# Block 0's two token halves issued together, its second gather behind the first, and all other loads held until the second half has landed

## The chip, the cores and the metric

The kernel runs on one core of one Trainium2 chip. The metric is the device time of one execution in microseconds (us). A core has five engines that each run their own instructions in order: TensorE (PE; its weight loads are shown as PEld), VectorE (DVE), ScalarE (ACT), GpSimd (POOL) and SyncE (SP). SP and GpSimd issue the transfers (DMAs) between the chip's large memory and the core's own; sixteen DMA engines carry them out. Engines wait for one another and for transfers by semaphores.

## The reference

There are 64 sequences of 64 tokens with 1024 numbers each (4096 tokens, 32-bit floats). Two layers with a residual are applied:

```
x = x + (x B[id0]^T) A[id0]                    # rank-16 adapter of the sequence, one of 64
logits = x Wr^T + 5 * onehot(id1)              # 8 experts
gates  = softmax of the top 2 logits, else 0
h      = x A1^T                                # 8 experts x rank 16 = 128 numbers
x = x + x W^T + 2 * (h * gates) B1
```

`W` is 1024 x 1024 and costs most of the arithmetic.

## The kernel before

The tokens stand in the large memory with the features outermost (`xT`). The kernel takes them in eight blocks k of 512 tokens; a block is two tiles `x(k,0)` and `x(k,1)` of 512 features each (1 MB). Two blocks make a super-block s, and the product with `W` plus the identity (which brings the residual) is made for a super-block with Strassen's scheme in two levels: seven outer products of quarter matrices, each in turn from seven inner ones, so that sums of tokens (`t`, `ti`) and of weights (`m`, `s`) are formed ahead of the matmuls. In super-block 0 the first outer product is made without the inner level (`pw`). The combined weights are written to the large memory (`s_kept`) in super-block 0 and read back by the other three.

Ahead of the products each block goes through these steps, all with the names that the profile shows:

- `gather` (GpSimd, indirect DMA): the block's adapter rows, `gb` (of `in_b`) and `ga` (of `in_a`), 0.5 MB each.
- `turn`: transposes of `gb` on TensorE (`pt`), copied by ScalarE to `bt`.
- `project`: `pb` from `bt` and the tokens, in two steps, one for each half of the features; VectorE masks it to `bx`.
- `adapt`: `px` from `ga` and `bx`, which VectorE adds to the tokens (`x<-px,x`).
- `rows`: `ph` from the tokens and `a1_sb` (expert rows and router), copied to `h` by ScalarE.
- `gates`: some twenty small VectorE operations from `l<-h,bias` to the gated rows `h<-h,s`.
- `weigh`: transposes of the gated rows (`pg`), copied to `hg`; the products read it with `b1_sb`.

The order of the instructions on every engine is made when the kernel is built. Each step is handed to `Plan.add` with the engines that it may run on, an estimated duration, what it reads and writes, a due time `at`, and for a transfer its size `kb`. `Plan.order` plays the steps through with these estimates and always takes, on the engine that can start first, the ready step that is due first. `LAND`, `KB` and `GATHER` are its estimates for transfers:

```
if st["kb"]:
    moved = max(moved, clock[e]) + st["kb"] / self.KB
    end[n] = (moved if e == "SP" else clock[e] + self.GATHER) + self.LAND
```

`behind` is a condition of the planner alone: the step is placed after the start of another. A real hold is made in another way: a small GpSimd copy writes one column of the tile that a transfer will fill, so that the transfer has to wait for that copy, and the copy reads from a tile that has to land first. The kernel before has two of them. In `load`, the tile `x(0,1)` is held by a copy from `x(0,0)`, whose load is cut into two transfers of 0.5 MB. In `consts`, `a1_sb` is held by a copy from `gb` of block 0. SP issues its transfers in order, so all that is planned behind `a1` waits with it. GpSimd runs in order too, so a gather that stands behind such a copy waits as well. The transfers of SP share eight semaphores in turn, and one of them can be issued only when the transfer eight places earlier has landed.

SP's order at the start is: the ids of the first layer, `x(0,0)` in two parts, `wr` (the router) and `ids1` (the ids of the second layer, one row sent to all partitions), `x(0,1)`, `a1`, two of the sixteen pieces `w(i,j)` of `W`, `x(1,0)`, `x(1,1)`, the other fourteen (first `w(1,0)` and `w(1,1)`), `b1`. GpSimd's is: gather `gb(0)`, hold of `x(0,1)`, gather `ga(0)`, copy of `wr` into `a1_sb`, hold of `a1_sb`, gathers `gb(1)` and `ga(1)`, then sums of weights. The list of calls is:

```
for k, at in ((0, -60), (1, -42)):
    load(k, 0, at)
    gather(k, "gb", b0, at - 1)
    load(k, 1, at)
    gather(k, "ga", a0, at)
    if k == 0:
        consts()
```

Of the kernel before, what the change touches and what calls it, by code (L numbers as in the profile page):

```python
# [14 lines left out]
P = 128  # L15
# [18 lines left out]
class Plan:  # L34
# [10 lines left out]
    LOOK = 0.2  # L45
    LAND = 1.8
    KB = 350.0
    GATHER = 1.5
    AHEAD = 6.0
    PACE = {"DVE": 0.36, "POOL": 0.73}  # L50
    SET = {"SP": 1.2, "DVE": 3.1, "POOL": 2.9}
# [13 lines left out]
    def order(self):  # L65
# [65 lines left out]
        while ready:  # L131
# [23 lines left out]
# [3 lines that stand above are left out]
            where[n] = e  # L158
# [23 lines left out]
def kernel(  # L182
# [52 lines left out]
    TB = 512  # L235
# [5 lines left out]
    HC = NC // 2  # L241
# [15 lines left out]
    act, pool, sp = Pinned(tc, nc.scalar), Pinned(tc, nc.gpsimd), Pinned(tc, nc.sync)  # L257
# [6 lines left out]
    plan = Plan(slots, {"l"})  # L264
# [7 lines left out]
    def new(tag, shape, name):  # L272
        return pools[tag].tile(shape, F32, tag=tag, name=name)
# [24 lines left out]
    a1_sb = const.tile([P, NC, P + E], F32, name="a1_sb")  # L298
# [13 lines left out]
    def consts():  # L312
        plan.add({"SP": 0.4}, lambda e: sp.dma_start(wr_c, wr), [], [("wr_c",)], -53, kb=8)
        plan.add(
            {"SP": 0.4}, lambda e: sp.dma_start(ids1_sb, ids1[0:1, :].to_broadcast([P, NB])),
            [], [("ids1",)], -53, kb=32,
        )

        def hold(e):

            pool.tensor_copy(a1_sb[:, 0, :1], made["gb", 0][:, :1])

        plan.add({"POOL": 0.2}, hold, [(("gb", 0),)], [("a1",)], -56)
        plan.add({"SP": 0.4}, lambda e: sp.dma_start(a1_sb[:, :, :P], a1), [], [("a1",)], -45, kb=512)
        plan.add({"SP": 0.4}, lambda e: sp.dma_start(b1_sb, b1), [], [("b1",)], -29, kb=512, behind=[("a1",)])

        def spread(e):
            pool.tensor_copy(a1_sb[:, :, P:], wr_c)

        plan.add({"POOL": 0.3}, spread, [("wr_c",)], [("wr",)], -45)  # L330
# [24 lines left out]
    made = {}  # L355

    def part(t, cs=range(HC), gs=range(NG)):
        return [(t, c, g) for c in cs for g in gs]
# [7 lines left out]
    def load(k, i, at):  # L366
        t = ("x", k, i)

        held = (k, i) == (0, 1)

        def hold(e):

            made[t] = new("q", [P, HC, TB], f"x_{k}_{i}")
            pool.tensor_copy(made[t][:, 0, :1], made["x", 0, 0][:, 0, :1])


        cuts = ((0, HC // 2), (HC // 2, HC)) if (k, i) == (0, 0) else ((0, HC),)

        def fn(c0, c1):
            if not held and c0 == 0:  # L380
                made[t] = new("q", [P, HC, TB], f"x_{k}_{i}")
            sp.dma_start(
                made[t][:, c0:c1],
                xT[(i * HC + c0) * P : (i * HC + c1) * P, k * TB : (k + 1) * TB].rearrange(
                    "(c p) t -> p c t", p=P
                ),
            )

        if held:
            plan.add(  # L390
                {"POOL": 0.2}, hold, part(("x", 0, 0), [0]), part(t), at, [("q", t)]
            )
        for c0, c1 in cuts:
            plan.add(
                {"SP": 0.5}, lambda e, c0=c0, c1=c1: fn(c0, c1),
                [], part(t, range(c0, c1)), at, [("q", t)] * (not held and c0 == 0),
                kb=256 * (c1 - c0), behind=[("a1",)] * (k == 1) + [(t, 0, 0)] * (c0 > 0),
            )

    def gather(k, tag, table, at):  # L400
        def fn(e):
            made[tag, k] = new(tag, [P, D], f"{tag}_{k}")
            pool.indirect_dma_start(
                out=made[tag, k],
                out_offset=None,
                in_=table,
                in_offset=bass.IndirectOffsetOnAxis(ap=idx[:, k : k + 1], axis=0),
            )

        plan.add(  # L410
            {"POOL": 1.1}, fn, [], [((tag, k),)], at, [(tag, (tag, k))], kb=512,
            behind=[(("x", 0, 1), 0, 0)] * ((tag, k) == ("ga", 0)) + [("a1",)] * (k == 1) + [(("px", 1, 1, 0),)] * (k > 1),
        )

    def turn(k, g, at):
# [261 lines left out]
    POOL = {"POOL": 1.25}  # L677
# [367 lines left out]
# [7 lines that stand above are left out]
# [9 lines left out]
    for s in range(NSUP):  # L1061
        k0 = 2 * s
        a0_ = s * SLOTS
        if s == 0:
            late(0, -14)
        late(k0 + 1, a0_ + 4 * (s > 0))
        token_sum(s, 3, a0_ + 3)
        token_sum(s, 2, a0_ + 5)
        token_sum(s, 4, a0_ + (25 if s == 0 else 7))
        token_sum(s, 1, a0_ + 20)  # L1070
        products(s)
        if s + 1 < NSUP:
            k0, k1 = k0 + 2, k0 + 3
            gather(k0, "gb", b0, a0_ + 8)
            gather(k0, "ga", a0, a0_ + 9)
            load(k0, 0, a0_ + 9)
            load(k0, 1, a0_ + 14)
            early(k0, a0_ + 17)
            late(k0, a0_ + 23)
            gather(k1, "gb", b0, a0_ + 22)  # L1080
            gather(k1, "ga", a0, a0_ + 23)
            load(k1, 0, a0_ + 22)
            load(k1, 1, a0_ + 29)
            early(k1, a0_ + 32)
# [48 lines left out]
```

## Time and profile before

| | |
|---|---|
| median of 3 runs | 521.96 us (521.91 to 522.75) |
| the profiled execution | 521.59 us, span 519.8 us, granted TensorE clock 1.00 |
| busy: PE, PEld | 504.9 us (97%), 439.3 us (85%) |
| busy: DVE, ACT, POOL | 300.9 us (58%), 41.1 us (8%), 170.0 us (33%) |
| bytes moved | 99.19 MB, mean 191 GB/s |
| first matmul | starts at 9.72 us |

The span runs from the first to the last instruction of the profiled execution; times in the lines of the profile count from its start. A line of the timeline or of the chain of waits begins with start and duration; a group of equal instructions is drawn together, with its count. Nearly all instructions stand under line 29, since one helper issues them, so they are told apart by their tiles. In a list of waits, the numbers are the total, the count and the longest. In the lines by DMA queue, q1 carries what SP issues and q0 the gathers; the numbers are packets, MB, and the time that the packets took as a share of sixteen engines.

### The profile page before, as it was taken

The page shows a single profiled execution, that of the slowest core. Times are in us where ns is not written, and L with a number is a line of the kernel's source. Part 1 is how long each engine was busy: PE and PEld are TensorE (multiplying, and loading weights), DVE is VectorE, ACT ScalarE, POOL GpSimd, SP SyncE. Part 2 cuts the span into 40 slices and gives each one's busy share as a digit, 9 for nine tenths or more (in the row PEclk, how much of TensorE's full clock was granted, in tenths as well). Part 3 has the DMA queues.
Part 4 walks back from the last instruction along what each step waited for, and adds up shares of the span by engine and source line. Part 5 has one row for each costly group of instructions (what it writes and reads, how often), then busy time and mean ns, then how long its engine had stood idle before and what let it go on. Part 6 is the DMA issues. An engine that isn't in the chain of part 4 may idle for free.

```text
span 519.8 us, 8542 instructions
## 1 busy us (share of the span) xinstructions
PE 504.9 (97%) x3432; PEld 439.3 (85%) x3432; DVE 300.9 (58%) x572; ACT 41.1 (8%) x81; POOL 170.0 (33%) x141
## 2 busy tenths in 40 slices
PE   2999999999999999999999999999999999999996
PEld 2857988888888988898888998889888898888885
DVE  0699998986953383526684256435486418433632
ACT  1111100002000100012000100000200010000000
POOL 4072067170332144124233313312423322433300
PEclk9999999999999999999999999999999999999999
DMA  7999276799566269716565537744546633610122
GB/s 263 370 367 381 103 263 221 276 326 342 194 202 203 63 194 317 238 61 204 182 224 186 159 101 212 269 149 124 163 161 202 204 95 107 204 62 0 56 104 83
DMA packets 54247, 99.19 MB, mean 191 GB/s; under 512 B 4928, under 2 KB 11072, under 8 KB 54208
## 3 DMA queue, kind: packets, MB, share of 16 engines
q1 hardware_dynamic: 51904, 90.26, 51.6%
q0 software_dynamic: 2304, 8.39, 4.8%
q8 instruction: 27, 0.44, 0.3%
q14 instruction: 12, 0.10, 0.0%
HBM read 69.01 MB, written 29.62 MB: 190 GB/s over the span
## 4 chain that ended last, share of the span: by engine, by line
PE 96%; DMA 2%; DVE 0%; issue 0%; SPq 0%; POOL 0%
PE pa L29 39%; PE pb L29 38%; PE ph L29 11%; PE px L29 3%; PE pw L29 3%; DMA x<-in_xT 2%; PE pt L29 1%; PE pg L29 1%; DVE o L29 0%; SPq L29 0%; DVE bx L29 0%; POOL x L29 0%
## 5 line engine op out<-in xcount | busy, mean ns | idle before, releaser
L29 PE MATMUL pa<-ti,s 128*128 128x256 f32 x432 | 102.5, 380 | 0.0
L29 PE MATMUL pb<-ti,s 128*128 128x256 f32 x384 | 95.8, 380 | 0.0
L29 PEld LDWEIGHTS pa<-ti,s 128*128 128x128 f32 x432 | 80.8, 190 | 11.2 <-issue 0.2
L29 PEld LDWEIGHTS pb<-ti,s 128*128 128x128 f32 x384 | 72.1, 190 | 10.0
L29 PEld LDWEIGHTS ph<-a_sb,x 128*128 128x128 f32 x512 | 62.6, 190 | 1.5 <-issue 0.4
L29 PE MATMUL ph<-a_sb,x 128*128 128x136 f32 x512 | 63.1, 279 | 0.2 <-issue 0.2
L29 POOL TENSOR_TENSOR ti<-x,ti 128x512 f32<-128x512 f32 x24 | 32.2, 1340 | 78.0 <-PE pb L29 77.1
L29 DVE TENSOR_TENSOR o<-pb,o 128x512 f32<-128x512 f32 x47 | 32.4, 690 | 36.1 <-PE pb L29 21.7
L29 PE MATMUL pa<-x,s 128*128 128x256 f32 x216 | 51.9, 379 | 0.0
L29 POOL TENSOR_TENSOR ti<-t,ti 128x512 f32<-128x512 f32 x18 | 25.7, 1429 | 71.0 <-PE pb L29 61.3
L29 POOL TENSOR_TENSOR ti<-x 128x512 f32<-128x512 f32 x24 | 30.8, 1282 | 55.4 <-PE pb L29 41.8
L29 PEld LDWEIGHTS pa<-x,s 128*128 128x128 f32 x216 | 40.1, 190 | 5.3 <-issue 0.3
L29 DVE TENSOR_TENSOR x<-px,x 128x512 f32<-128x512 f32 x64 | 39.8, 684 | 6.8 <-PE px L29 6.8
L29 PE MATMUL pa<-t,s 128*128 128x256 f32 x168 | 41.0, 380 | 0.0
L29 POOL TENSOR_TENSOR ti<-t 128x512 f32<-128x512 f32 x18 | 24.4, 1358 | 42.9 <-PE pb L29 33.4
L29 PEld LDWEIGHTS pa<-t,s 128*128 128x128 f32 x168 | 31.6, 190 | 4.5 <-issue 0.4
L29 DVE TENSOR_TENSOR o<-pa,u 128x512 f32<-128x512 f32 x32 | 22.0, 688 | 20.8 <-PE pa L29 20.1
L29 DVE TENSOR_TENSOR u<-pb,u 128x512 f32<-128x512 f32 x21 | 14.5, 689 | 25.1 <-ACT u L29 20.7
L29 POOL TENSOR_TENSOR s<-w,w 128x512 f32<-128x512 f32 x12 | 17.0, 1418 | 36.0 <-DVE w L29 36.0
L29 PE MATMUL pb<-hg,b_sb 128*128 128x256 f32 x96 | 28.6, 379 | 0.0
L29 DVE TENSOR_TENSOR o<-pa,v 128x512 f32<-128x512 f32 x15 | 10.3, 690 | 25.9 <-PE pa L29 25.9
L29 DVE TENSOR_TENSOR v<-pa,u 128x512 f32<-128x512 f32 x16 | 11.0, 689 | 22.3 <-PE pa L29 22.1
(113 smaller groups left out, 609.5 us busy)
## 6 DMA issues: line engine op xcount, KB each, us to landing
s<-s_kept SPq DMA_DIRECT2D x147, 256.0 KB
x<-in_xT SPq DMA_DIRECT2D x15, 1024.0 KB
out_T<-o SPq DMA_DIRECT2D x30, 512.0 KB
s_kept<-s SPq DMA_DIRECT2D x28, 256.0 KB
s_kept<-w SPq DMA_DIRECT2D x18, 256.0 KB
w<-in_w SPq DMA_DIRECT2D x16, 256.0 KB
x<-in_xT SPq DMA_DIRECT2D x2, 512.0 KB
out_T<-o SPq DMA_DIRECT2D x4, 256.0 KB
```

What stands on the lines that cost most here:

```text
L29: return self._tc.keep_in_program_order(f(*args, **kwargs))
```

## The change

`x(0,0)` is loaded by one transfer instead of two, and the load of `x(0,1)` loses its hold, so that both are issued one after the other. The gather `ga(0)` is no longer placed behind the start of `x(0,1)`. The hold on `a1_sb` copies from `x(0,1)` instead of `gb(0)`, so what is queued behind it waits until that half has landed. The planner's estimate for a gather goes from 1.5 to 3.0. In the built order GpSimd now issues `ga(0)` right behind `gb(0)`, then the hold, the copy of `wr`, `gb(1)`, `ga(1)`; SP issues `x(0,0)`, `x(0,1)`, `wr`, `ids1`, `a1` and the rest as before.

The instructions of every engine are otherwise the same in number, but the plan orders some of them anew. Up to about 65 us these differ: on VectorE, the identity added to `w(1,1)` stands ahead of block 0's gates, and in block 1 all four `ti` and one `o` stand ahead of the gates, not after them; on TensorE, block 0's `pg` and the first `pa` stand ahead of block 1's second `px`, the first `pb` of product 2 ahead of block 1's `ph`, and block 1's `pg` behind block 2's `pt`. Later than that, the orders are the same but for two stores that change places.

```diff
-    GATHER = 1.5
+    GATHER = 3.0
...
         def hold(e):
 
-            pool.tensor_copy(a1_sb[:, 0, :1], made["gb", 0][:, :1])
-
-        plan.add({"POOL": 0.2}, hold, [(("gb", 0),)], [("a1",)], -56)
+            pool.tensor_copy(a1_sb[:, 0, :1], made["x", 0, 1][:, 0, :1])
+
+        plan.add({"POOL": 0.2}, hold, part(("x", 0, 1), [0]), [("a1",)], -56)
...
     def load(k, i, at):
         t = ("x", k, i)
 
-        held = (k, i) == (0, 1)
-
-        def hold(e):
-
+        def fn(e):
             made[t] = new("q", [P, HC, TB], f"x_{k}_{i}")
-            pool.tensor_copy(made[t][:, 0, :1], made["x", 0, 0][:, 0, :1])
-
-
-        cuts = ((0, HC // 2), (HC // 2, HC)) if (k, i) == (0, 0) else ((0, HC),)
-
-        def fn(c0, c1):
-            if not held and c0 == 0:
-                made[t] = new("q", [P, HC, TB], f"x_{k}_{i}")
             sp.dma_start(
-                made[t][:, c0:c1],
-                xT[(i * HC + c0) * P : (i * HC + c1) * P, k * TB : (k + 1) * TB].rearrange(
+                made[t],
+                xT[i * HC * P : (i + 1) * HC * P, k * TB : (k + 1) * TB].rearrange(
                     "(c p) t -> p c t", p=P
                 ),
             )
 
-        if held:
-            plan.add(
-                {"POOL": 0.2}, hold, part(("x", 0, 0), [0]), part(t), at, [("q", t)]
-            )
-        for c0, c1 in cuts:
-            plan.add(
-                {"SP": 0.5}, lambda e, c0=c0, c1=c1: fn(c0, c1),
-                [], part(t, range(c0, c1)), at, [("q", t)] * (not held and c0 == 0),
-                kb=256 * (c1 - c0), behind=[("a1",)] * (k == 1) + [(t, 0, 0)] * (c0 > 0),
-            )
+        plan.add(
+            {"SP": 0.5}, fn, [], part(t), at, [("q", t)], kb=1024, behind=[("a1",)] * (k == 1)
+        )
...
         plan.add(
             {"POOL": 1.1}, fn, [], [((tag, k),)], at, [(tag, (tag, k))], kb=512,
-            behind=[(("x", 0, 1), 0, 0)] * ((tag, k) == ("ga", 0)) + [("a1",)] * (k == 1) + [(("px", 1, 1, 0),)] * (k > 1),
+            behind=[("a1",)] * (k == 1) + [(("px", 1, 1, 0),)] * (k > 1),
         )
```

## The prediction

> **What bounds the kernel now.** I read the table of busy time first: TensorE (PE) 504.9 of 519.8 us. Then TensorE's waits, for the whole span:
>
> ```profile
> PE pt L29 <- DMA gb<-in_b,idx: 9.7, 1, 9.7
> PE pb L29 <- DMA x<-in_xT: 0.6, 1, 0.6
> PE px L29 <- DVE bx L29: 0.4, 1, 0.4
> PE ph L29 <- issue: 0.2, 1, 0.2
> ```
>
> All four lie in the first 19 us; from `ph` on TensorE never waits again. So the end moves by what the start gains and by any new hole later, one for one. The chain of waits gives the start:
>
> ```profile
> 4.78 8.80 DMA x<-in_xT
> 13.59 0.14 issue
> 13.72 1.11 PE pb L29 x32
> 14.86 0.30 DVE bx L29
> 15.20 2.07 PE px L29 x64
> 17.27 1.18 PE pt L29 x8
> ...
> 18.64 7.65 PE ph L29 x64
> ```
>
> Block 0's second half x(0,1), held until the first quarter of tokens has landed, takes 8.8 us for 1 MB. GpSimd's timeline gives the gathers of block 1, which the change delays:
>
> ```profile
> 9.64 0.18 POOL L29 COPY a_sb<-gb 128x1 f32<-128x1 f32 x1 [2.95 <-DMA gb<-in_b,idx]
> 9.97 0.97 POOL L29 DMA_INDIRECT gb<-in_b,idx  x1
> ```
>
> The list of transfers gives gb(0) 6.7 us from issue to landing, gb(1) 6.4, each ga 8.0: gb(0) lands at 9.58, gb(1) at 16.37, ga(0) at 12.92. Why x(0,1) is slow shows in the DMA split by queue between 5.3 and 8 us (145 GB/s in all, 353 in the three us before):
>
> ```profile
> DMA packets 282, 0.39 MB, mean 145 GB/s; under 512 B 195, under 2 KB 195, under 8 KB 282
> ...
> q0 software_dynamic: 84, 0.34, 54.4%
> q1 hardware_dynamic: 198, 0.05, 7.4%
> ```
>
> The 256-byte rows of wr and ids1 stand in SP's queue ahead of x(0,1) and trickle for 2.7 us; none of x(0,1) moves before 8.
>
> A second place matters because the order written after the change differs there, between 40 and 65 us. VectorE (DVE) and TensorE meet:
>
> ```profile
> 44.53 2.48 DVE L29 TENSOR_TENSOR x<-px,x 128x512 f32<-128x512 f32 x4
> ...
> 54.74 0.19 DVE L29 TENSOR_TENSOR l<-h,bias 128x32 f32<-128x32 f32 x1
> ...
> 63.11 0.69 DVE L29 TENSOR_TENSOR w<-m,w 128x512 f32<-128x512 f32 x1
> ...
> 63.86 1.70 PEld L29 LDWEIGHTS pa<-t,w 128*128 128x128 f32 x8
> ```
>
> VectorE is busy almost without a gap, and the combined weights that `pa` loads at 63.86 are finished at 63.80. Nothing is spare at that point.
>
> **What the skill says.** "DMA: Bandwidth & Descriptors", section Queues, rings and completion order: each DMA engine goes round its queues packet by packet. The trace agrees: from 10.5 to 12 us q0 (4 KB packets) and q1 (2 KB) moved 103 and 116 packets, so the gathers took 0.40 of 0.62 MB. The same page, Anatomy of one DMA, fits a GpSimd transfer as 2.0 us plus bytes over 436 GB/s, 3.2 us for a 0.5 MB gather; the trace has 6.4 to 8.0, and I use the trace. "SBUF — State Buffer", section Who interferes with whom: a VectorE operation with two SBUF inputs contends with GpSimd operations that read SBUF. The trace agrees: a `l<-s,l` of 0.19 us (56.09) takes 1.28 at 28.59 beside a GpSimd sum.
>
> **Part by part.**
>
> 1. *x(0,0) as one load, x(0,1) right behind, no hold.* Removes one SP issue (0.46 us), one GpSimd copy (0.18). x(0,1) is issued near 1.7 instead of 4.78; wr and ids1 move behind it, 0.4 us later at SP. GpSimd is free, so ga(0) goes at about 4.1 instead of 4.92. x(0,1) now shares the rings with gb(0) from 5.3 on, when q0's first packets appear. One DMA engine's share of both halves is 64 packets of 2 KB; 16 engines at 400 GB/s need 2.1/0.40 = 5.3 us, begun at 2.4. Add gb(0)'s 0.52/0.41 = 1.3 us and part of ga(0): last packets 9.0 to 10.3, landing some 0.9 later (the tail that x(0,1) shows now, thinning from 12.5, landing at 13.59). I take **10.6** (9.9 to 11.3), 3 us earlier than now.
>
> 2. *gb(0) without the trickle.* ga(0) today needs about 3.2 us from first packets (about 9.7) to landing against 2 KB packets; gb(0) begun at 5.3 then lands at **8.5**, not 9.58. TensorE: `pt` 8.6; `pb`'s first half 1.87 later as now (9.72 to 11.59), 10.5; it takes 1.54, to 12.0. The second half needs x(0,1), there since 10.6: no wait. 1.12, then 0.34 for `bx`: `px` starts at **13.5** instead of 15.20 and ends at 15.5. It needs ga(0): queued behind gb(0), about 8.7 plus 3.2, plus up to 1 us for the trickle that now falls on it: 12 to 13, just covered.
>
> 3. *Other loads held until x(0,1) has landed.* The hold on `a1_sb` moves from gb(0)'s landing (9.64) to x(0,1)'s (10.65). Queued behind it on GpSimd: the copy of wr (which used to run at 6.45, 0.24 us), gb(1), ga(1); on SP: a1, two w, x(1,0), x(1,1), fourteen more w, b1. gb(1) is issued at 10.65 + 0.34 (hold to next issue, as 4.58 to 4.92) + 0.24 = **11.2** instead of 9.97. Its landing: 2.4 to first packets (as gb(0), 2.88 to 5.3) plus 3.2, or today's 6.4 to 6.7. I take 5.7: **16.9** (16.3 to 17.9). TensorE runs in order, so block 1's `pt` stands after `px` and waits from 15.5 until 16.95, where it started at 17.20. **Gain 0.25 us**, not the 1.7 that `px` gains. `ph` follows by 1.4 as now. a1 needs to land by 18.4; it is issued at 10.9, 1.1 later than now, and behind the trickle: hidden by `pt`'s wait.
>
> 4. *Block 1's tokens and w.* The DMA pause of 5.3 to 8 is exchanged for one from about 10.3 to 12.5. x(1,1) is needed at about 27. SP issues the w that waits for its semaphore at 26.45 now; I take the same, cover 0.7 us. w(1,1), which SP's issue at 27.97 shows landed just before, now stands on VectorE ahead of `l<-h,bias` (26.75): that gate chain starts near 28.4 and is drawn into GpSimd's eight sums. Counted by hand with the durations at 28.6 to 38.7, `h` is gated at 41.2 instead of 40.3. `pg` at 43.4 covers that; if w(1,1) is over 0.7 us later, no longer.
>
> 5. *GATHER 3.0 reorders 40 to 65 us.* `pg` (0.54) and `pa` (1.62) move ahead of block 1's second `px`, and six `pb` (2.5) ahead of `ph`. TensorE's sum is the same, but VectorE's `x<-px,x` can start only after them. TensorE: 43.34 + 0.54 = 43.9, `pa` to 45.5, its result at 45.9; VectorE takes it (0.6), `m` (0.6), so `x<-px,x` starts at **47.1**, not 44.53. From there with the rows now: four adds 2.5, eight token sums 4.8, four `ti` 2.6, one `o` 0.6: `l<-h,bias` at 57.6 (54.74 now). Gates and gated rows 4.6, `o`, `m` and two `w` 2.7: **64.9**, against 63.8 now, where two `ti` and the `o` (1.9) stood after the gates. `pa` waits for it: **a loss of 1.05 us** (0.6 if a gap of VectorE is counted twice; 1.8 if item 4's cover fails). The `pg` before it waits 0.6 of that. Later order is the same, with both engines shifted alike.
>
> Sum: −0.25 + 1.05 = **+0.8 us**. The profiled execution is 521.59 (span 519.8), 0.37 under the median 521.96, which I move: **522.7**. A difference under 0.2%, 1.04 us, can't be told from no change here.
>
> **Rivals.**
>
> - *A, likeliest (0.47):* as summed, most of the early gain used up by the wait for gb(1), the rest and more by VectorE's order. 520.9 to 523.0. Against it: the landing times carry 0.7 us of doubt.
> - *B, slower (0.38):* gb(1) keeps its 6.7 us and x(0,1) lands at 11.3, since the gathers take two packets' bytes for each of its own. gb(1) is issued at 11.9, lands at 18.6: `pt` 1.4 later than now, plus 1.05: +2.5, 524.4. It decides from a gb(1) landing of 17.2 on, where the start gains nothing and +1.05 remains. For it: no gather in the trace took under 6.4. Against it: gb(0) suffered from the trickle, gb(1) stood behind ga(0); both reasons go.
> - *C, faster (0.15):* VectorE has slack that I miss, for instance GpSimd's sums overlapping less, so that item 5 costs nothing, and gb(1) lands at 15.5 to 16. Then −1.2 to −1.7: 520.5. The full −1.7 is the limit: `px` ends no earlier than 15.5. Against it: 63.80 beside 63.86.
> - *D:* the change doesn't bring x(0,1) earlier, because SP's queue is served late: it needs x(0,1) after 13; then B's sum and more. Included in B.
>
> **Numbers.** Faster 0.15, same 0.47, slower 0.38. The range leaves out B's tail and the extreme of C: 520.9 to 524.1. A alone with its own doubts: 522.0 to 523.0.
>
> **What would show it.** Right: x(0,1) landed near 10.6 and no wait of `pb` for x; `px` near 13.5; a new wait of `pt` for gb of 1 to 2 us, ending near 17; a wait of `pg` or `pa` for VectorE at 62 to 65 us. Wrong: block 1's `pt` right after `px` (item 3), or no TensorE wait after 40 us (item 5), or a wait of `pb` for block 1's x at 27 (item 4).

## The result, and the profile after

The changed kernel took 526.84 us (median of six, 525.49 to 527.78) beside 521.93 us for the kernel before: a ratio of 1.0088, 95% interval 1.0070 to 1.0106. It is 4.9 us slower, outside the range that was forecast (520.9 to 524.1). A second series of the same kernel (`a2_again`, 17 times) gave 525.50 beside 521.70, ratio 1.0073 (1.0053 to 1.0093); eleven of those times lie between 523.5 and 525.7, six between 526.7 and 527.7. The two profiles, of a 527.78 us execution and of one of 524.96 us, show both kinds.

The list of TensorE's waits, for the longer of the two (total, count, longest):

```profile
PE pt L29 <- DMA gb<-in_b,idx: 14.1, 2, 10.8
PE px L29 <- DVE bx L29: 0.4, 1, 0.4
```

Before, `pt` waited once, 9.7 us. Now it waits twice: 10.8 us for block 0's `gb` and 3.3 us, which is new, for block 1's. The wait of `pb` for tokens is gone. The chain of waits (start, duration, what) says where the second wait comes from:

```profile
2.21 10.29 DMA wr_c<-in_wr
12.49 0.05 issue
12.55 0.24 POOL a_sb L29
12.79 0.15 issue
12.93 8.36 DMA gb<-in_b,idx
21.29 0.14 issue
21.43 1.77 PE pt L29 x8
23.20 8.51 PE ph L29 x64
31.71 1.88 PE pb L29 x64
```

Block 1's `pt` starts at 21.43, 17.20 before. Its gather lands 8.36 us after its issue (6.4 before), and the issue itself, 9.97 before, is at 12.93. GpSimd's timeline has the reason, in the brackets (idle before, and what ended it):

```profile
11.72 0.18 POOL L29 COPY a_sb<-x 128x1 f32<-128x1 f32 x1 [6.49 <-DMA x<-in_xT]
12.55 0.24 POOL L29 COPY a_sb<-wr_c 128x64 f32<-128x64 f32 x1 [0.64 <-DMA wr_c<-in_wr]
12.93 0.97 POOL L29 DMA_INDIRECT gb<-in_b,idx  x1
```

The hold is released at 11.72 (9.64 before). Behind it stands the copy of `wr`, which has to wait for `wr` to land, and only then comes the gather. (In what follows, `pt(1)`, `pb(1)` and so on are the steps of block 1.)

`pt` and `ph` are also longer than before, 1.77 and 8.51 us against 1.18 and 7.65. The split by stretches (start and end, length, busy PE, PEld, DVE, ACT, POOL, then the granted TensorE clock, DMA share, GB/s) shows the clock at half from about 21.6 to 25.0:

```profile
20.00:21.00 1.00, 0.00 (x0) 0.00 (x0) 1.00 (x3) 0.00 (x0) 0.00 (x0) 1.00 1.04 412
21.00:22.00 1.00, 0.57 (x4) 0.61 (x5) 1.00 (x2) 0.00 (x0) 0.00 (x0) 0.81 1.02 387
22.00:23.00 1.00, 1.00 (x6) 0.80 (x4) 0.92 (x5) 0.56 (x1) 0.00 (x0) 0.50 1.04 401
...
25.00:26.00 1.00, 1.00 (x11) 1.00 (x10) 1.00 (x2) 0.00 (x0) 0.00 (x0) 0.98 1.05 368
```

The Trainium skill, page "TensorE: Matmul & The Clock Gate", Part 1: The HAM clock gate, states that TensorE falls to half its clock after about one window of 3.4 us without work and needs about as long at work to come back. This trace agrees: 3.3 us of waiting, a fall 3.5 us after TensorE's last work (18.14), then 3.4 us at 0.50.

In the other profile, `a2_again`, TensorE's timeline has a shorter wait and no fall:

```profile
16.68 2.07 PE L29 MATMUL px<-bx,ga 32*128 32x128 f32 x64 [0.38 <-DVE bx L29]
19.83 1.07 PE L29 MATMUL pt<-ident,gb 128*128 128x128 f32 x8 [1.08 <-DVE x L29]
```

There `gb(1)` was issued at 12.75 and landed at 19.69, 0.14 before `pt` started. The list puts this wait down to VectorE, one of whose additions ended just then; but `pt(1)` starts 0.13 or 0.14 after the landing in `after`, `e2_old_order` and `e5_cut` too, and where the gather had landed earlier (`e6_copy_behind`, `e13_copy_old_order`) it doesn't wait for the additions. In the longer one fifteen of the sixteen DMA engines had finished `gb(1)` by 20.26 and the last came at 21.29.

That the fall of the clock goes with the long times shows in more than these two profiles. The mean granted clock of every execution is on record: 0.995 to 0.997 in the ten executions of 526.7 us or more of the two series, 0.998 to 1.000 in the thirteen shorter ones.

Two points on TensorE sum the whole span up: the start of block 1's `pb` (all that the start costs lies ahead of it) and the time from there to the first `pa<-x,s` (the order of 40 to 65 us lies in it). The last four rows are kernels of the next section.

| kernel | start of pb(1) | from there to `pa<-x,s` | span |
|---|---|---|---|
| before | 26.22 | 39.72 | 519.8 |
| after | 31.64 (+5.42) | 40.42 (+0.70) | 526.0 (+6.2) |
| a2_again | 28.82 (+2.60) | 40.43 (+0.71) | 523.2 (+3.4) |
| e1_order | 26.14 (-0.08) | 40.79 (+1.07) | 521.1 (+1.3) |
| e2_old_order | 28.66 (+2.44) | 39.70 (0.0) | 522.3 (+2.5) |
| e6_copy_behind | 27.25 (+1.03) | 40.42 (+0.70) | 521.6 (+1.8) |
| e13_copy_old_order | 27.78 (+1.56) | 39.71 (0.0) | 521.4 (+1.6) |

In every row the two differences add up to that of the span within 0.1 us, but for `e1_order`, where 0.3 us lie later. So there are two costs in the changed kernel: the start, 2.6 to 5.4 us, and the order, 0.7.

### The profile page after: what moved, and what is told of

It reads as the page before. It is cut to its first block, busy times and chain, and to the rows that moved or that the text cites. A ratio compares the mean times of both kernels' runs of the same rounds, so it can differ in the third digit from the quotient of the medians.

```text
span 526.0 us, 8534 instructions
## 1 busy us (share of the span) xinstructions
PE 507.3 (96%) x3432; PEld 441.2 (84%) x3432; DVE 298.0 (57%) x572; ACT 40.9 (8%) x81; POOL 169.4 (32%) x140
## 4 chain that ended last, share of the span: by engine, by line
PE 95%; DMA 4%; SPq 0%; DVE 0%; issue 0%; POOL 0%
PE pa L29 39%; PE pb L29 37%; PE ph L29 11%; PE px L29 3%; PE pw L29 3%; DMA wr_c<-in_wr 2%; DMA gb<-in_b,idx 2%; PE pt L29 1%; PE pg L29 1%; SPq L29 0%; DVE o L29 0%; POOL a_sb L29 0%
## 5 line engine op out<-in xcount | busy, mean ns | idle before, releaser
L29 PEld LDWEIGHTS pa<-ti,s 128*128 128x128 f32 x432 | 80.7, 190 | 11.2 <-issue 0.2
L29 POOL TENSOR_TENSOR s<-w,w 128x512 f32<-128x512 f32 x12 | 17.0, 1419 | 35.5 <-DVE w L29 20.9
L29 PE MATMUL pb<-x,s 128*128 128x256 f32 x96 | 23.9, 381 | 0.0
```

Of the source, the lines that this page charges most:

```text
L29: return self._tc.keep_in_program_order(f(*args, **kwargs))
```

## The experiments

All were timed beside the kernel before on the same chip; ratios are to it, with 95% intervals. The diffs show the lines that matter: the text behind a # names the experiment, and "..." stands for code that is left out.

**The two costs apart: e1_order, e2_old_order.**

```diff
-    GATHER = 1.5          # e1: the kernel before with the new order alone
+    GATHER = 3.0
-    GATHER = 3.0          # e2: the changed kernel with the old order
+    GATHER = 1.5
```

> The kernel before with GATHER = 3.0 as the only edit: TensorE and ScalarE take the changed kernel's order, all loads and gathers stay as before. Theory T (the start costs most: block 1's gather comes late, TensorE waits 3.3 us for it and then runs 3.4 us at half clock; the order adds little): pa waits some 0.4 us for VectorE's combined weights and starts 0.7 us later than before, 522.6 us in all (+0.7; the prediction said +1.05). Rival R (the order of 40 to 65 us is the cause): +3 us or more. Rival 0 (the order costs nothing, the 0.7 us seen comes from the shifted start): 522.0.

> The changed kernel with GATHER = 1.5 again: the engines' orders of the kernel before, the new loads and holds. Theory T: gb(1) still lands near 21.3, pt of block 1 waits over 3 us, the granted clock falls to half at 22 to 25 us, pb(1) starts 5.4 us later than before; in all about +4.2 over the kernel before, 526.1. Rival R (the order): back to about 522.

Measured: 522.86 (+1.3; ratio 1.0027, 1.0014 to 1.0040) and 524.94 (+3.4; 1.0066, 1.0051 to 1.0082). The sum is 4.6; the change cost 4.9 and, in its second series, 3.8. The order is a cost of its own, though in e1_order VectorE takes one `m` behind block 1's gates that the changed kernel takes ahead of them. TensorE's waits in e1_order name it:

```profile
PE pa L29 <- DVE w L29: 0.6, 1, 0.6
```

Rival R falls. In e2's profile, of its shortest time, `gb(1)` landed at 19.53 and the clock did not fall, against the expectation; as in `a2_again`, a short time goes without it.

**When gb(1) is issued: e3_gathers_first, e6_copy_behind.**

```diff
-            behind=[("a1",)] * (k == 1) + [(("px", 1, 1, 0),)] * (k > 1),     # e3
+            behind=[(("px", 1, 1, 0),)] * (k > 1),
-        plan.add({"POOL": 0.3}, spread, [("wr_c",)], [("wr",)], -45)          # e6
+        plan.add({"POOL": 0.3}, spread, [("wr_c",)], [("wr",)], -45, behind=[(("ga", 1),)])
```

(In e6 the line is called after block 1's gathers are in the plan.)

> The changed kernel with block 1's two gathers no longer behind the hold on a1 (GpSimd issues gb(0), ga(0), gb(1), ga(1), then the hold and the copy of wr); the other loads stay held until x(0,1) has landed. Theory T (it is the time at which gb(1) is issued): gb(1) lands before 16, no wait of pt over 1 us, no fall of the clock, and pb(1) starts within 1 us of the kernel before; what stays is the order's 0.7 us and x(0,1) landing 1 to 2 us later for the added gather bytes: about 523 (+0.5 to +1.5). Rival H (the hold on the other loads, a1 and w coming late, costs the time whatever the gathers do): stays at 525 to 526.

> The changed kernel with GpSimd's copy of wr (0.24 us, behind a wait of 0.64 us for wr's landing) moved behind block 1's two gathers; no other instruction moves. Theory T (block 1's pt waits for gb(1), and gb(1)'s landing follows its issue): gb(1) issued near 12.05 instead of 12.93, landed 0.9 us earlier, the time 0.9 us shorter than the changed kernel's, more if the shorter wait keeps the clock up. Rival H (gb(1)'s landing is set by the loads of a1, w and x that SP issues from 11.9 on, not by its own issue): lands within 0.3 us of where it landed, no gain.

e3: 524.20 (1.0048, 1.0035 to 1.0061), a miss above the 523 or so that was expected. In its profile, of its shortest time (523.26), `gb(1)` was there at 13.4, no clock fell, and `pb(1)` started at 26.50, only 0.28 later than before, though a1 was issued only at 11.56: rival H falls. (a1 landed at 16.76, and at 16.29 in the changed kernel, against 17.07 in e1_order, whose loads are those of before.) The rest of that profile is order: with the gather early, the planner put part of `pt` ahead of `px`, and `ph`, with no `pt` between it and `px`, started 1.2 us after `px`; at the first `pa<-x,s` the kernel was 1.34 late. The 0.9 us from this profile's time to the median is not explained.

e6: 523.50 (1.0026, 1.0014 to 1.0038), 2.0 us under `a2_again` of the same series for moving one copy of 0.24 us; none of its 21 times is over 523.94, so the long ones are gone. The issue of `gb(1)` came 0.79 earlier (12.75 to 11.96), but its landing 2.26 earlier (19.69 to 17.43). `pt` no longer waits; TensorE's timeline of e6:

```profile
16.23 2.07 PE L29 MATMUL px<-bx,ga 32*128 32x128 f32 x64 [0.38 <-DVE bx L29]
18.23 1.19 PE L29 MATMUL pt<-ident,gb 128*128 128x128 f32 x8
```

Why 2.26 for 0.79? The transfers by queue between 12.5 and 16 us (packets, MB, share of sixteen engines' time), first e6, where all 0.52 MB of a1 and then half of the gather moved:

```profile
q1 hardware_dynamic: 1040, 0.52, 51.0%
q0 software_dynamic: 66, 0.27, 19.3%
```

then `a2_again`, where q0, the gathers' queue, has no line at all:

```profile
q1 hardware_dynamic: 1284, 0.77, 76.4%
```

In `a2_again` SP had issued the first w (12.39) before the gather (12.75), and a1 and that w, 0.77 MB, moved before its first packet at 16.7; in e6 only a1 had been issued, and the first packet came at 15.3. Two more profiles repeat it: first packet at 16.5 and landing at 19.53 in e2_old_order, 15.0 and 17.42 in e13_copy_old_order. In these profiles a gather's packets start when most of what was under way at its issue has moved.

**Block 0's own gather: e4_halves_only, e5_cut, e8_other_queue, e11_hold_on_issue.**

```diff
-        held = (k, i) == (0, 1)                                              # e4, from before
+        held = False
-        cuts = ((0, HC // 2), (HC // 2, HC)) if (k, i) == (0, 0) else ((0, HC),)
+        cuts = ((0, HC),)
+        cuts = ((0, HC // 2), (HC // 2, HC)) if (k, i) == (0, 0) else ((0, HC),)   # e5, from after
-            sp.dma_start(                                                    # e8, from after
+            (act if (k, i) == (0, 1) else sp).dma_start(
-            pool.tensor_copy(made[t][:, 0, :1], made["x", 0, 0][:, 0, :1])   # e11, from before
+            pool.tensor_copy(made[t][:, 0, :1], ident[:, :1])
```

(In e11 the copy is placed behind the issue of `gb(0)`.)

> The kernel before with x(0,0) in one load and x(0,1) issued right behind it, no hold between them; a1 and the rest are still held by gb(0)'s landing, GATHER stays 1.5. Tells whether issuing the halves together delays gb(0) itself. If the gather's packets stand behind what SP has already queued (theory Q): gb(0)'s first packets come near 7.2 and it lands near 10.6 as in the changed kernel, 1 us later than before; gb(1) is issued near 11.0; pt of block 0 1 us later, px still earlier or equal; about +0.5 to +1.5 (522.5 to 523.5). If they don't (rival): gb(0) lands by 9.6 and x(0,1) near 11.5, px starts 1 to 1.5 us earlier and the time is 0 to 1.5 us shorter.

> The changed kernel with x(0,0) cut in two loads of 0.5 MB again, x(0,1) still issued at once behind them, everything else as changed. In the traces of the changed kernel and of e4_halves_only the 1 MB loads moved only 0.31 and 0.30 MB by 4.0 us, the kernel before 0.57 MB. Theory S (one long load starts slower, and all behind it, gb(0) too, is shifted by it): 0.5 MB or more by 4.0 us, gb(0)'s first packets near 6.6 and landing near 10.0, x(0,1) near 11.0, gb(1) issued and landed 0.6 us earlier: 0.5 to 0.9 us faster than the changed kernel. Rival Q (the gather's packets wait for what SP has queued before them, whatever its cut): gb(0) lands at 10.5 again and the time stays within 0.3 us of the changed kernel's.

> The changed kernel with x(0,1) issued on ScalarE's queue instead of SP's, near 1.2 to 1.7 us; nothing else moves, wr and ids1 now stand right behind x(0,0) on SP's queue. Theory Q (the first packets of a gather come only after what stands in SP's queue ahead of it): gb(0)'s first packets near 5.3 to 6 as in the kernel before, not 7.0 to 7.25, and gb(0) lands before 9.6. Rival B (it waits for all bytes in flight, whatever the queue): first packets at 7.0 or later, landing at 10.3 or later. In both x(0,1) lands at 11 to 12, so that the hold and gb(1) come as in the changed kernel and the time falls by 1 us at most.

> The kernel before with one edit: x(0,1) is released by GpSimd as soon as gb(0)'s gather has been issued (a copy of one column of the identity behind it), near 4.3 us, instead of when the first quarter of tokens has landed, 4.78. Theory B (a gather's first packets wait for the token bytes in flight when it is issued): gb(0) starts at 5.3 and lands near 9.6 as before, since x(0,1) is issued after it; x(0,1) lands 0.5 us earlier or at the same time; 521.3 to 521.9, no change beyond 0.5 us. Rival P (what counts is which data are ready first at the DMA engines): gb(0) starts at 7 or later and lands at 10.3 or later, and the time grows by 0.5 to 1.5 us.

e4: 522.50 (1.0015, 1.0007 to 1.0023). `gb(0)`'s first packet came at 7.37 and it landed at 10.60 (5.33 and 9.58 before). e5: 525.57 (1.0075, 1.0053 to 1.0097), the same as `a2_again`; 0.48 MB had moved by 4.0 us, so the cut does speed the start of the transfer, but the gather's first packet stayed at 7.36: theory S falls as a cost. (In its profile `gb(0)` landed only at 11.91, and the last DMA engine of x(0,1) came 1.8 us after the fifteenth.) e8: 524.89 (1.0060, 1.0042 to 1.0078). On another queue x(0,1) landed early, at 6.43, but x(0,0) at 9.50, and the gather's queue from 7 to 8 us shows one packet:

```profile
q0 software_dynamic: 1, 0.00, 1.0%
```

So theory Q (SP's queue) falls and rival B holds: nearly all 2.1 MB of tokens had moved before it, 1.7 in the kernels with one queue. The gather was also issued later here, at 3.55, so its first packet at 7.9 is 4.4 us after its issue, as in those kernels; it landed at 12.27. (`gb(1)` came late here too, since GpSimd waited 4.36 us for `wr` ahead of it.) e11: 522.01 (1.0008, 1.0000 to 1.0016). With x(0,1) issued at 4.23, after the gather at 2.89, the first packet is at 5.47 and `gb(0)` lands at 9.22 (9.58 before). What delays `gb(0)` is x(0,1) being under way ahead of it.

**The rows of wr and ids1: e7_rows_behind, e10_rows_after_a1, e12_rows_last.**

```diff
-        plan.add({"SP": 0.4}, lambda e: sp.dma_start(wr_c, wr), [], [("wr_c",)], -53, kb=8)
+        plan.add({"SP": 0.4}, lambda e: sp.dma_start(wr_c, wr), [], [("wr_c",)], -53, kb=8, behind=[(("x", 0, 1), 0, 0)])   # e7
+        plan.add({"SP": 0.4}, lambda e: sp.dma_start(wr_c, wr), [], [("wr_c",)], -45, kb=8, behind=[("a1",)])               # e10, e12
```

(`ids1` the same way, all from the kernel before; in e10 and e12 these loads are also written behind a1's hold and load. e12 is e10 with the edit of e11.)

> The kernel before with SP's loads of wr and ids1 (256-byte rows) issued behind x(0,1) instead of ahead of it, and so GpSimd's copy of wr behind block 1's gathers; GATHER stays 1.5, x(0,1) is still held by the first quarter of x(0,0). Tests the second step of the prediction, that these rows hold up gb(0) and x(0,1) between 5.3 and 8 us. If they do: over 300 GB/s from 5.5 to 8 us, gb(0) lands near 8.5, x(0,1) near 11 to 12, px up to 1.5 us earlier, a1's hold and gb(1) 1 us earlier: 0.5 to 1.2 us faster than before. If it is the gather itself that starts slowly (rival): the hole between 5.3 and 8 us stays, gb(0) lands at 9.3 to 9.8, and the time stays within 0.3 us of before.

> As e7_rows_behind (the kernel before, rows of wr and ids1 behind x(0,1)), but with these rows further back, behind a1's load: only a1 stands behind x(0,1) in SP's queue until gb(1) is issued. Tells what makes the hole in the transfers, which moved to 6.5 to 9 us in e7_rows_behind. If it is the rows being made ready in SP's queue (theory R): no hole, x(0,1) lands by 11, px starts by 13, and the time is 0.5 to 2 us shorter than before (519.7 to 521.2). If it is that x(0,1) starts into an empty queue and in step with a gather (theory E): the hole stays at 6.5 to 9, x(0,1) lands near 14, 524 to 526 as in e7_rows_behind.

> e10_rows_after_a1 (rows of wr and ids1 behind a1) with the same edit, x(0,1) released by gb(0)'s issue, near 4.3 instead of 5.1 us. If the hole at 6.5 to 9 us there comes from x(0,1) starting into an empty queue (theory E), x(0,1) issued 0.8 us earlier finds x(0,0) still under way: no hole, x(0,1) lands by 11.5, gb(0) by 8.5, px by 13.5, and the time is 0.5 to 2 us shorter than before (519.5 to 521). If a load that starts beside a starting gather creeps in any case (rival), the hole stays, x(0,1) lands near 14 to 15, and the time is 524 to 526.

e7: 525.29 (1.0066, 1.0048 to 1.0085), 3.6 us slower where 0.5 to 1.2 faster was expected. Without the rows ahead of it `gb(0)` landed at 7.38, 2.2 us earlier than before. But x(0,1) then crept, `pb` waited 3.7 us for it, and the clock fell. e10: 525.13 (1.0061, 1.0040 to 1.0082), with no rows in the way at all: the hole stays, so theory R falls. The rates (GB/s, one number per half microsecond from 0 on), first of e10, then of e12, which differs only in issuing x(0,1) at 4.23 instead of 5.10 and, right behind it, `ga(0)` at 4.36 instead of 5.23:

```profile
GB/s 0 0 0 8 62 254 270 328 414 418 406 397 393 266 139 152 188 221 270 299 311 299 327 330 339 340 401 398 403 389 415 372 326 274 326 333 353 373 381 383
```

```profile
GB/s 0 0 0 8 82 262 274 336 402 397 438 406 360 266 307 360 418 393 389 426 418 297 248 299 336 373 381 319 204 261 356 365 289 299 361 367 424 369 389 377
```

From 7 to 9 us the first moves 139 to 221 GB/s, the second 307 to 418, as theory E says; why such a start is slow stays open. In e12 x(0,1) landed at 12.55, `pb(1)` started 1.0 us earlier than before and the profiled span was 1.0 shorter. The median, 521.73, was not: ratio 0.9992 (0.9972 to 1.0013).

**The clock itself: e9_busy_wait.**

```diff
+            if (k, cs[0]) == (0, HC):                 # e9, from e7
+                idle = new("b", [P, PER, P], "idle")
+                for _ in range(24):
+                    pe.transpose(idle[:, 0, :], ident, ident)
```

> The kernel of e7_rows_behind with 24 useless transposes of the identity on TensorE, put where it waited 3.7 us for x(0,1), between the halves of block 0's pb; they add work and remove none, no load moves. There px took 3.80 us instead of 2.07, at a granted clock of 0.50 from 16 to 20.6 us. Theory C (the idle wait itself makes the clock fall): with the wait cut to about 1 us the clock stays at 1.00, px takes 2.1 us, and the kernel is 1.5 to 2 us faster than e7_rows_behind (525.3), near 523.6. Rival (the clock falls for another reason, or the records are wrong on it): same time as e7_rows_behind or longer, px 3.8 us.

Measured: 523.34 (1.0032, 1.0018 to 1.0045), against 525.29 (1.0066, 1.0048 to 1.0085) for e7; the intervals lie apart. TensorE's timeline, first e7, then e9:

```profile
14.71 1.94 PE L29 MATMUL pb<-x,bt 128*32 128x128 f32 x32 [3.72 <-DMA x<-in_xT]
17.05 3.80 PE L29 MATMUL px<-bx,ga 32*128 32x128 f32 x64 [0.40 <-DVE bx L29]
```

```profile
16.35 1.08 PE L29 MATMUL pb<-x,bt 128*32 128x128 f32 x32 [1.31 <-DMA x<-in_xT]
17.84 2.07 PE L29 MATMUL px<-bx,ga 32*128 32x128 f32 x64 [0.40 <-DVE bx L29]
```

In e9's profile x(0,1) came 1.6 us later, and `px` still ended 0.9 earlier. The clock's own records tell how. In e7 TensorE was given full speed at 10.51 and lost it at 13.93, in the wait, until 20.75. In e9 it was given full speed at 13.06, among the transposes (they follow one another every 0.21 us up to there, every 0.11 after), and kept it through the last 1.3 us of waiting. So work without use in the wait leaves TensorE at full speed when `px` comes: theory C.

**The order once more, and a better version: e13_copy_old_order, a2_again, e12_again, e14_hold_right.** e13 is e6 with `GATHER = 1.5`; `a2_again` and `e12_again` are unchanged.

> e6_copy_behind (the changed kernel, copy of wr behind block 1's gathers) with GATHER = 1.5, the order of the kernel before on TensorE, VectorE and ScalarE. e6_copy_behind took 523.5, and its pb(1) started 1.0 us later than before. If the order costs what e1_order's median says (1.3): 522.2. If it costs what the traces of after and e1 show (0.6 to 0.7): 522.8. If nothing: 523.5.

> The changed kernel once more, unchanged, for a second profile beside these runs: its six times ran from 525.5 to 527.8 and the one profiled was the longest. Theory V (gb(1)'s landing varies from execution to execution by some slow DMA engines, and the longer wait costs TensorE's clock on top): a profile of a time near 525.5 shows gb(1) landed by 19.8, a wait of pt under 2.5 us and no fall of the clock. Rival: the fall of the clock is in every execution, and the times differ elsewhere.

> e12_rows_last once more, unchanged. Its profile started pb(1) 1.0 us earlier than before and was 1.0 us shorter, but the times ran from 520.6 to 523.9. If the gain is there in most executions: median 520.9 to 521.3 beside 521.6 for before. If landings vary so much that it is lost: 521.6 to 522.

> e12_rows_last with the hold on a1 released by x(0,1)'s landing as in the change, but with block 1's two gathers issued by GpSimd ahead of the hold (at about 5.6 and 6.9 us), and GATHER = 5.0, with which the planner keeps TensorE's order of the kernel before. If the gathers in flight leave x(0,1) its place (it is issued before them): x(0,1) lands by 12.5, px by 14.2, gb(1) by 13, a1 by 16, the time 0.5 to 1.2 us shorter than before (520.4 to 521.1). If a1 and wr, issued only near 12.5, become the next wait (of ph, needed at 17.6): 521.5 to 523.5.

```diff
-    GATHER = 1.5                                                         # e14, from e12
+    GATHER = 5.0
...
-            pool.tensor_copy(a1_sb[:, 0, :1], made["gb", 0][:, :1])
+            pool.tensor_copy(a1_sb[:, 0, :1], made["x", 0, 1][:, 0, :1])
...
-            behind=[(("x", 0, 1), 0, 0)] * ((tag, k) == ("ga", 0)) + [("a1",)] * (k == 1) + ...
+            behind=[(("x", 0, 1), 0, 0)] * ((tag, k) == ("ga", 0)) + [(("ga", 0),)] * (k == 1) + ...
...
-            [("l", pt)] + [("bt", bt)] * (g == 0),
+            [("l", pt)] + [("bt", bt)] * (g == 0), behind=[(("px", 0, 1, 0),)] * (k == 1),
```

e13: 522.63 (1.0022, 1.0015 to 1.0029), 0.9 under e6 by the medians of two series; their intervals overlap, and the traces (table above) put the order at 0.7 in these kernels. `a2_again` is told above: theory V holds, in the two profiles and in the granted clocks on record. e12_again: 522.39 (1.0010, 0.9997 to 1.0022); five of sixteen times lie between 520.4 and 520.8, the others between 521.9 and 524.9. Its profile, of a 522.78 us execution, shows why, beside that of e12_rows_last (520.60); first e12_rows_last, then e12_again:

```profile
12.69 1.08 PE L29 MATMUL pb<-x,bt 128*32 128x128 f32 x32 [0.94 <-DMA x<-in_xT]
14.17 2.07 PE L29 MATMUL px<-bx,ga 32*128 32x128 f32 x64 [0.40 <-DVE bx L29]
```

```profile
12.96 1.93 PE L29 MATMUL pb<-x,bt 128*32 128x128 f32 x32 [1.03 <-DMA x<-in_xT]
15.30 3.12 PE L29 MATMUL px<-bx,ga 32*128 32x128 f32 x64 [0.40 <-DVE bx L29]
```

The same instructions take 1.9 us longer: TensorE had not yet come up to speed. The clock column says 1.00 there in both, but only because it stands at 1.00 until the trace has a record of the clock; the first record, of full speed, comes at 12.35 in e12_rows_last and at 17.56 in e12_again. The same page of the skill says that the window runs freely, so that the point at which TensorE warms up differs from run to run; these two profiles fit that. e14: 523.56 (1.0049, 1.0029 to 1.0068): x(0,1) landed at 13.60 beside the four gathers (12.55 and 12.83 in e12's profiles), and a1 at 18.25. `pb(1)` started 1.47 later than before, and from there to `pa<-x,s` it took 0.44 longer, so the planner did not keep the order of before quite as expected. No version was shown faster than the kernel before.

## Why the prediction was wrong, step by step

1. *x(0,1) near 10.6 (9.9 to 11.3):* 11.67, and 11.44 in `a2_again`. 1.9 us of the 3 came. The direction held; one 1 MB load moved only 0.31 MB by 4.0 us where two of 0.5 MB had moved 0.57, which the step did not have; how much of the lateness that makes is not shown.
2. *gb(0) at 8.5, "shares the rings with gb(0) from 5.3 on":* **failed.** It landed at 10.67 (10.44), 1.1 later than before. The step took the round of the queues, packet by packet, from the Trainium skill's page "DMA: Bandwidth & Descriptors", section Queues, rings and completion order, to hold from the issue on. The trace shows that only between packets already under way; the gather got its first packet at 7.3. By the queue split from 6.5 to 7.5 us of the changed kernel it had eight so far:

```profile
q0 software_dynamic: 8, 0.03, 8.4%
```

   `px` started at 16.06 (16.68), not 13.5. The rest of that gap is TensorE at half speed: `pb`'s halves were counted at 1.54 and 1.12, as in the kernel before, where full speed came at 12.59, 2.9 us after TensorE's first work. In the changed kernel it came at 14.80 (16.69), 4.0 (6.1) us after, and the two halves took 2.96 (3.86) together.
3. *gb(1) issued at 11.2, landed at 16.9, gain 0.25:* **failed, and most of the loss is here.** The hold came 1.1 later than the step's 10.65; the copy of `wr`, counted at its 0.24, waited 0.64 more for `wr`, whose rows now stood behind both halves; so the issue was at 12.93 (12.75). The landing time, taken as 5.7, was 8.36 (6.94): SP's a1 and first w were under way by then, and in the longer execution the last DMA engine came another 1.0 late. That 5.7 was not wrong in itself: e6 has 5.5 with the copy out of the way. `pt` came 2.6 to 4.2 late instead of 0.25 early, and in the long executions the clock, to which the prediction gave no term, added 0.6 on `pt` and 0.9 on `ph`.
4. *Block 1's tokens and w covered:* held, with more room than was counted on: TensorE came to `pb(1)` only at 31.64 (28.82) and did not wait for them.
5. *The order costs 1.05, `pa` waits for the weights:* the mechanism held, the size was 0.7. The +1.07 of e1_order agrees with 1.05 in part by luck, for there one more `m` stands behind the gates than the step counted. In the changed kernel VectorE's `x<-px,x` starts 20.6 us after `pb(1)` (18.3 before; 20.9 forecast). The sign that the step named, a wait of `pg` or `pa`, stands in no list of TensorE's waits there, but its weight loads (PEld) have it, where the kernel before has none (63.86, the line in the prediction):

```profile
69.99 1.59 PEld L29 LDWEIGHTS pa<-t,w 128*128 128x128 f32 x8 [0.39 <-DVE w L29]
```

   In the starts of the matmuls the 0.7 is split into four delays of 0.3 us or less, at `pg` and at three `pa`.

So the sum +0.8 was off in one term above all, the start: -0.25 forecast, +2.6 to +5.4 found. Rival B was the right mechanism with the right deciding point (a landing after 17.2), but its 18.6 was too early; it took "gb(0) suffered from the trickle, gb(1) stood behind ga(0); both reasons go" as evidence against, and a new reason, the loads under way, took their place. The trickle itself was half right: the rows did hold up `gb(0)` (e7: 7.4 without them), but the hole is not theirs (e10).

## What to carry to other kernels

When a transfer is moved ahead, ask what is issued after it and will now be served after it: here a gather paid 1 us for the load put in front of it and a second gather paid more. Walk the in-order queue behind a moved hold one instruction at a time; a 0.24 us copy whose own input had become late cost 2 us. And price a wait of TensorE of some 3.3 us (the shortest after which the clock fell here) with what follows it at half clock, not by its length alone. A delay that TensorE's list of waits doesn't show can still stand in the waits of its weight loads.

## What the runs showed of the hardware that was not expected

- A gather's first packet came 2.2 to 2.6 us after its issue behind 1 MB of tokens and 4.3 to 4.5 us behind 2 MB, whether these stood on one queue (after, e4) or on two (e8); for `gb(1)` 3.1 to 3.3 us behind a1 alone, 3.5 to 4.0 behind a1 and one w. Why it isn't served in turn is open, and so is whether the 1 MB delayed it at all.
- With a load of 1 MB issued 0.9 us later (5.10 against 4.23), when the tokens before it were nearly through, all transfers together moved 139 to 221 GB/s from 7 to 9 us instead of 307 to 418.
- Waits of TensorE of 3.3, 3.7 and 4.4 us (after, e7, e10) were each followed by a clock of 0.50; waits of 1.1 and 1.3 us (`a2_again`, e9) were not. The fall came 3.5, 2.9 and 3.7 us after TensorE's last work, and half speed lasted 3.4, 6.8 and 6.8 us. In these traces every stretch at one clock between two changes is a multiple of 3.41 us. 24 useless transposes in such a wait made a kernel about 2 us faster.
- TensorE came to full speed 2.9 us after its first work in the kernel before, 4.4 and 9.4 us after it in two executions of e12, and that moved e12's time by 1.9 us.
